# Butterfly weights of the first layer: two rotating buffers become three, the load is asked for in the middle of a step, and three bias loads move behind them

## The chip, the cores and the metric

The kernel runs on one core of a Trainium2 chip. A core has five engines that follow their own instruction streams: TensorE (PE, with weight loads shown apart as PEld), VectorE (DVE), ScalarE (ACT), GpSimd (POOL) and SyncE (SP), which in this kernel issues nearly all DMA transfers. Times are device microseconds from the first to the last instruction of one execution. The kernel before was run three times: 4143.59, 4148.38 and 4153.01 us; its time is the median, 4148.38 us. One further execution was profiled.

## The reference, cut to what matters

Four layers act on x, 4096 tokens of 128 numbers. Each is `x + s * silu(g)` with s from an attention block and g from a feed-forward block. Only the first layer matters here. Its attention has 16 heads of 8 numbers, a causal mask over 256 tokens, and two relative-position terms that look up products of q and k with position vectors by the clipped distance of two tokens:

```python
relpos = jnp.clip(qi[None, :] - qi[:, None], -WIN + 1, 0) + (WIN - 1)
c2p = jnp.einsum('bnhd,whd->bhnw', q, rk)[:, :, qi[:, None], relpos]
p2c = jnp.einsum('bnhd,whd->bhwn', k, rq)[:, :, relpos, qi[None, :]]
logits = (c2c + c2p + p2c) / math.sqrt(hd * scale_factor)
```

Its feed-forward block has butterflies between two dense matrices. A butterfly of 512 numbers has 9 steps; step `stage` mixes pairs that stand 2**stage apart with four weights a pair:

```python
h = butterfly(jnp.einsum('bsd,dh->bsh', x, W_exp) + b_exp, up_weights, 512)
h = butterfly(jax.nn.gelu(h + up_bias, approximate=False), down_weights, 512)
y = jnp.einsum('bsh,hd->bsd', h, W_con) + b_con + down_bias
# one step:
na  = w[..., 0, 0] * a + w[..., 0, 1] * b
nb2 = w[..., 1, 0] * a + w[..., 1, 1] * b
```

Up to the gelu everything is linear, and so is everything behind it.

## The kernel before

Because of that linearity the kernel never applies a butterfly to tokens. It applies the nine steps once to the rows of `W_exp`, once to the single row `b_exp`, and, transposed and in reverse order, to the rows of `W_con` transposed; from then on the block is two dense products. That makes 27 steps, numbered 0 to 26 here: 0 to 8 for `wexp` (128 rows of 512), 9 to 17 for `bexp` (one row), 18 to 26 for `wconT` (128 rows). A step is done on POOL in two halves of three instructions (`stage`, L160 to L180): two products of 128x256 (L171), then their sum (L174). Its 1024 weights are loaded from DRAM by the SP queue and spread over the 128 partitions (`fetch`, L189 to L195, 512 KB written; one row for steps 9 to 17). The weight load of step k is called w(k) here. Loads and intermediate rows lie in the buffer `xn`, which holds the normalised input of the layer: `room` is a view of it, free after its transposes. Two weight buffers rotate: step n asks for w(n+1) before its own first product, and so w(k) has to wait until the last product of step k-2 has read the same buffer.

While POOL does this, the first layer's attention (`attn0`) runs on all engines. Its 64 items are numbered n = 4b + m: batch b of 16, and a group m of four heads. An item is scored, shifted, softmaxed and mixed: TensorE forms the scores of four heads (L382), adds straightened position terms (L393 to L395), DVE adds the second position term and takes the row maximum (L398 to L400), ACT takes exp (L403), TensorE turns the result (L409), ACT and DVE copy it out of PSUM (L412, L414), and TensorE mixes (L423) one item later. The position terms go through DRAM, where a slanted write does the lookup:

- **Band store (b, hh, i)**, for hh, i in 0, 1: TensorE forms a product (L346), ACT copies it to `a_es` (L354), and SP writes it slanted (L357), twice: first a `cs` write, then a `pc` write, 256 KB each. `a_es` has two buffers in all, so ACT's copy for one band store waits until the DMA writes of the band store before it have read theirs.
- **Band load (b, hh)**: SP reads four pieces back, two for `a_p` (L362, 768 KB, and L363, 512 KB) and two for `a_c` (L364, L365). `a_p` has two buffers: the load for (b, hh) waits until POOL's copies have read the load two before it.
- **Straightening copies** of item n: eight copies on POOL, two for each head (L373, L374), from `a_p`; the next `project_qk` adds four products on POOL (L326).

The band stores of batch b+1 stand in items 4b (h = 0 and 1) and 4b+1, its band loads in items 4b+2 and 4b+4. `next(aside, None)` puts one half of a butterfly step into the program after each item, and a loop behind the last item takes what is left. The engine of TensorE keeps the order in which the program is written (`manual_schedule` names PE alone). For all other engines and for the SP queue the framework lays down an order when the program is built, from its own estimates of when operands are ready. Each engine and the SP queue then follow their order strictly; an instruction that waits holds back everything behind it on the same engine or queue.

At the end, `done` (L212 to L227) adds the biases: `bf_bs` from the `bexp` row and `upb` (L215), and `bdn`, the sum of `bcon` and `dnb` on DVE (L226). Before the change these three are loaded at the start of the layer (L210), and the sum `bdn` stands early in DVE's order.

In short, for the SP queue: weight loads and band transfers share one queue, and weight loads wait for POOL.

Of the kernel before, what the change touches and what calls it, by code (L numbers as in the profile page):

```python
# [8 lines left out]
F32 = mybir.dt.float32  # L9
# [6 lines left out]
P = 128  # L16
# [17 lines left out]
class Net:  # L34
# [113 lines left out]
    def butterflies(self, c):  # L148

        nc, tc = self.nc, self.tc
        wup = c.tile([P, 512], F32, name="wup")
        wdn = c.tile([P, 4, D], F32, name="wdn")
        bup = c.tile([P, 4], F32, name="bup")
        bdn = c.tile([P, D], F32, name="bdn")
        room = self.xn.rearrange("p k d -> p (k d)")
        ws = [room[:, 1024 * i : 1024 * i + 1024] for i in range(2)]
        ys = [room[:, 2048 + 512 * i : 2560 + 512 * i] for i in range(2)]
        t = room[:, 3072:3584].rearrange("p (j n) -> p j n", j=2)  # L160
        ends = {"bexp": room[:1, 3584:4096], "wexp": wup}

        def stage(out, y, wt, s, down):
            step, rows = 1 << s, y.shape[0]
            w5 = wt[:rows].rearrange("p (n s i j) -> p n s i j", s=step, i=2, j=2)
            src = y.rearrange("p (n t s) -> p n t s", t=2, s=step)
            dst = out.rearrange("p (n t s) -> p n t s", t=2, s=step)
            for i in range(2):
                for j in range(2):
                    v = w5[:, :, :, j, i] if down else w5[:, :, :, i, j]  # L170
                    nc.gpsimd.tensor_tensor(  # L171
                        t[:rows, j, :].rearrange("p (n s) -> p n s", s=step), src[:, :, j, :], v, ALU.mult
                    )
                nc.gpsimd.tensor_tensor(  # L174
                    dst[:, :, i, :],
                    t[:rows, 0, :].rearrange("p (n s) -> p n s", s=step),
                    t[:rows, 1, :].rearrange("p (n s) -> p n s", s=step),
                    ALU.add,
                )
                yield  # L180

        def steps():
            plan = [
                (name, weights, s)
                for name, weights in (("wexp", "upw"), ("bexp", "upw"), ("wconT", "dnw"))
                for s in (range(8, -1, -1) if name == "wconT" else range(9))
            ]

            def fetch(n):  # L189
                name, weights, s = plan[n]  # L190
                w = self.a[weights][:, 1024 * s : 1024 * s + 1024]
                rows = self.a[name].shape[0]
                if rows > 1:
                    w = w.rearrange("o n -> (o n)").partition_broadcast(P)
                nc.sync.dma_start(ws[n % 2][:rows], w)  # L195

            fetch(0)
            for n, (name, _, s) in enumerate(plan):
                rows, q = self.a[name].shape[0], n % 9
                if q == 0:  # L200
                    y = ys[0][:rows]
                    nc.sync.dma_start(y, self.a[name])
                if n + 1 < len(plan):
                    fetch(n + 1)
                o = ends[name] if q == 8 and name in ends else ys[(q + 1) % 2][:rows]
                yield from stage(o, y, ws[n % 2][:rows], s, name == "wconT")
                y = o
            ends["wconT"] = y

        ub, b1, b2 = self.load(c, "upb"), self.load_bc(c, "bcon"), self.load_bc(c, "dnb")  # L210

        def done():  # L212
            with tc.tile_pool(name="bf", bufs=1) as sb, tc.tile_pool(name="bf_ps", bufs=1, space=PSUM) as ps:
                bs = sb.tile([1, 512], F32, name="bf_bs")
                nc.vector.tensor_tensor(bs, ends["bexp"], ub, ALU.add)  # L215
                pb = ps.tile([P, 4], F32, name="bf_pb")
                for j in range(4):
                    nc.tensor.matmul(
                        pb[:, j : j + 1], lhsT=bs[:, j * P : (j + 1) * P], rhs=self.ones[:1, :1], start=True, stop=True
                    )  # L220
                nc.vector.tensor_copy(bup, pb)
                pd = ps.tile([P, 4, D], F32, name="bf_pd")
                for j in range(4):
                    nc.tensor.transpose(pd[:, j, :], ends["wconT"][:, j * P : (j + 1) * P], self.ident)
                nc.vector.tensor_copy(wdn, pd)
                nc.vector.tensor_tensor(bdn, b1, b2, ALU.add)  # L226
            return wup, bup, wdn, bdn  # L227

        return steps(), done

    def attn0(self, c, w, bias, wv, wo, bv, bo, aside):
# [1821 lines left out]
```

## Time and profile before

| what | value |
|---|---|
| median of three runs | 4148.38 us (4143.59 to 4153.01) |
| profiled execution, its own time | 4153.89 us |
| its span | 4152.2 us, mean granted TensorE clock 0.95 |
| PE busy | 3626.3 us, 87% of the span |
| DVE / ACT / POOL busy | 72% / 51% / 46% |
| first layer's attention, first to last item's scores (L382) | 62.0 to about 738 us |
| butterfly steps on POOL (L171, L174) | 61.6 to 258.9 us |
| four items, from 16 to 20 (285.9 to 324.7 us) | 38.8 us |
| items 0 to 14 | 62.0 to 265.1 us, 14.5 us each |

The profile has a page for the whole span and answers for stretches of it. Busy time is counted for each engine; a waiting instruction is not busy. A line of a timeline gives the start, the busy time, the engine, the source line, the operation with what it writes and reads, how many were merged, and in brackets how long the engine had been idle before and what ended that. A line of the table of waits gives who waited for whom, the time in total, how often, and the longest. A line of windows gives, for one stretch, the busy time of PE, PEld, DVE, ACT and POOL with the number of instructions, then the granted TensorE clock, the share of the DMA engines' time and GB/s.

The SP queue's order of the program before, as it was built, in the stretch of the butterflies. S(b,hh,i) is a band store, L(b,hh) a band load with the source lines' last digit, w(k) a weight load, and in brackets the step whose last product it waits for:

```
w0, S(0,0,1), L(0,0), S(0,1,0), wexp, w1, S(0,1,1), L(0,1), w2[0], S(1,0,0), w3[1], w4[2], S(1,0,1),
L(1,0):23, S(1,1,0), L(1,0):4, S(1,1,1) with L(1,0):5, L(1,1):23, w5[3], w6[4], w7[5], w8[6], L(1,1):45,
w9[7], bexp[8], w10[8], S(2,0,0), w11[9], S(2,0,1) with L(2,0):2, w12[10], w13[11], L(2,0):3, S(2,1,0),
w14[12], S(2,1,1) with L(2,0):45, L(2,1):23, w15[13], w16[14], w17[15], w18[16], L(2,1):45, wconT[17], w19[17],
cs of S(3,0,0), w20[18], pc of S(3,0,0), w21[19], S(3,0,1), L(3,0):23, w22[20], w23[21], S(3,1,0),
L(3,0):4, S(3,1,1), L(3,0):5, L(3,1):23, w24[22], w25[23], w26[24], L(3,1):45, S(4,0,0), ...
```

POOL's order in the same stretch (k is a step with halves a and b, c(n.h) the two copies of item n and head h, K the four products of L326; a copy between two halves may stand between their instructions):

```
c0 c1 0ab 1ab c2.0 c2.1 K c2.2 c2.3 2ab 3a c3.0 3b c3.1 4ab c3.2 c3.3 c4 c5.0 5a c5.1 5b 6a c5.2 6b c5.3 7ab 8ab
c6.0 c6.1 K 9a c6.2 c6.3 9b 10ab 11ab c7.0 c7.1 12ab c7.2 13a c7.3 13b 14ab c8 c9.0 15a c9.1 15b 16a c9.2 16b c9.3 17ab
c10.0 c10.1 18a K 18b c10.2 19a c10.3 19b 20ab 21ab c11.0-2 22a c11.3 22b 23ab c12 24a c13.0 24b c13.1 25ab c13.2 26a c13.3 26b c14.0 ...
```

### The profile page before, as it was taken

Reading aid. Unit: us, or ns where it says so; the run is one execution under the profiler, and the core shown is the slowest. Engines: PE = TensorE matmul, PEld = TensorE weight load, DVE = VectorE, ACT = ScalarE, POOL = GpSimd, SP = SyncE. Lnnn points to the kernel's source line nnn. Section 1 sums busy time; section 2 is a strip of 40 time slices with the busy share of each in tenths; the row PEclk is TensorE's granted clock in tenths of the full one; section 3 lists DMA queues with packets and bytes.
Section 4 is the critical chain, followed back from the end, with each engine's and each line's share of the span. In section 5 each row is a group of like instructions: output and inputs, shape, how many; then the busy total and the mean of one; then the engine's idle time right before and its main releaser. Section 6 shows DMA issues by size and latency. Waiting matters only on the chain. (4 is left out here: it accounts for less than half of the span.)

```text
span 4152.2 us, 61413 instructions
## 1 busy us (share of the span) xinstructions
PE 3626.3 (87%) x21623; PEld 2323.1 (56%) x21623; DVE 2987.9 (72%) x6273; ACT 2126.9 (51%) x4623; POOL 1918.5 (46%) x1979
## 2 busy tenths in 40 slices
PE   5689999875999999999999999769788899899795
PEld 3467777543566666777777776546333333333353
DVE  5467767575888887666666667636888999999834
ACT  2356666642777775444545333223565665666322
POOL 5974444000444443433333100250789877777634
PEclk8899999986999999999999899979899999999998
DMA  8365554320000001000000300010111211121123
GB/s 301 126 212 182 195 194 175 42 78 6 1 1 1 1 1 42 1 1 1 1 1 1 115 1 1 7 35 1 65 66 66 84 64 66 75 82 62 52 81 100
DMA packets 87366, 268.90 MB, mean 65 GB/s; under 512 B 18176, under 2 KB 34088, under 8 KB 81555
## 3 DMA queue, kind: packets, MB, share of 16 engines
q1 hardware_dynamic: 80403, 255.46, 18.0%
q0 software_dynamic: 6656, 9.52, 0.7%
q8 instruction: 172, 2.82, 0.3%
q14 instruction: 135, 1.11, 0.1%
HBM read 192.96 MB, written 71.97 MB: 64 GB/s over the span
## 5 line engine op out<-in xcount | busy, mean ns | idle before, releaser
L1827 POOL TENSOR_TENSOR m_h<-m_B,m_dtu 128x1024 f32<-128x1024 f32 x256 | 597.5, 2358 | 108.2 <-PE m_y L1957 104.1
L1853 DVE TENSOR_TENSOR_SCAN m_h<-m_a,m_h 128x512 f32<-128x512 f32 x512 | 601.3, 1208 | 40.1 <-ACT m_a L1842 34.8
L1957 PE MATMUL m_y<-m_h,ident 128*128 128x512 f32 x1024 | 513.8, 631 | 24.0 <-DVE m_h L1953 23.5
L883 POOL TENSOR_TENSOR a_e<-a_e,a_sm 128x512 f32<-128x512 f32 x256 | 263.8, 1041 | 445.2 <-DVE a_sm L882 351.5
L1117 DVE SCALAR_TENSOR_TENSOR f_acc<-f_po,f_gate,f_acc 128x128 f32<-128x128 f32 x1024 | 287.6, 344 | 219.8 <-PE f_po L1112 152.3
L1112 PEld LDWEIGHTS f_po<-values_sb,f_h 128*128 128x128 f32 x2048 | 277.5, 198 | 207.9 <-issue 130.5
L1957 PEld LDWEIGHTS m_y<-m_h,ident 128*128 128x128 f32 x1024 | 184.1, 195 | 340.3 <-issue 246.1
L398 DVE TENSOR_TENSOR a_e<-a_s,a_c 128x384 f32<-128x384 f32 x256 | 216.3, 845 | 189.9 <-PE a_s L395 183.6
L1189 POOL TENSOR_TENSOR r_g<-r_t 128x256 f32<-128x256 f32 x256 | 183.5, 728 | 360.3 <-DVE r_t L1188 357.2
L1083 ACT ACTIVATE f_h<-f_ph 128x512 f32<-128x512 f32 x256 | 152.2, 596 | 384.4 <-PE f_ph L1081 310.9
L1112 PE MATMUL f_po<-values_sb,f_h 128*128 128x128 f32 x2048 | 282.3, 283 | 71.5 <-ACT f_h L1083 46.6
L1220 ACT ACTIVATE r_e<-r_s,r_mx 128x256 f32<-128x256 f32 x512 | 208.0, 474 | 260.9 <-DVE r_mx L1214 260.8
L1953 DVE TENSOR_TENSOR m_h<-m_h,m_C 128x1024 f32<-128x1024 f32 x256 | 307.1, 1200 | 26.0 <-PE m_C L1863 26.0
L1188 DVE TENSOR_TENSOR r_t<-r_pp,trig_sb 128x512 f32<-128x512 f32 x256 | 169.5, 683 | 207.5 <-PE r_pp L1179 206.3
L876 ACT ACTIVATE a_e<-a_e,a_mx 128x256 f32<-128x256 f32 x512 | 255.1, 500 | 54.6 <-DVE a_sm L882 48.2
L1081 PE MATMUL f_ph<-xnT_sb,keys_sb 128*128 128x512 f32 x512 | 273.6, 618 | 0.4 <-ACT f_gate L1048 0.4
L403 ACT ACTIVATE a_e<-a_e,a_mx 128x128 f32<-128x128 f32 (+1 forms) x512 | 218.6, 453 | 93.0 <-DVE a_mx L399 65.0
L1208 PE MATMUL r_s<-pe_sb,r_g 128*128 128x256 f32 x1024 | 260.7, 388 | 0.0
L373 POOL COPY a_st<-a_p 128x192 f32<-128x192 f32 x256 | 135.7, 532 | 243.5 <-PE a_s L394 160.9
L1842 ACT ACTIVATE m_a<-m_dt,bA_sb 128x510 f32<-128x510 f32 x256 | 170.9, 686 | 141.3 <-DVE m_h L1853 140.4
L1863 PE MATMUL m_C<-m_dbc,ident 32*128 32x512 f32 x512 | 149.1, 655 | 96.6 <-DVE m_h L1953 92.3
L1842 ACT ACTIVATE m_a<-m_dt,fA_sb 128x510 f32<-128x510 f32 x256 | 169.9, 685 | 101.3 <-DVE m_h L1853 100.4
(476 smaller groups left out, 8227.5 us busy)
## 6 DMA issues: line engine op xcount, KB each, us to landing
m_B<-m_rows SPq DMA_DIRECT2D x32, 2048.0 KB
a_p<-pc SPq DMA_DIRECT2D x32, 768.0 KB
a_c<-cs SPq DMA_DIRECT2D x32, 768.0 KB
cs<-a_es SPq DMA_DIRECT2D x64, 256.0 KB
pc<-a_es SPq DMA_DIRECT2D x64, 256.0 KB
a_p<-pc SPq DMA_DIRECT2D x32, 512.0 KB
a_c<-cs SPq DMA_DIRECT2D x32, 512.0 KB
cs<-bg SPq DMA_DIRECT2D x8, 768.0 KB
```

The lines of the kernel that those rows point to most:

```text
L403: nc.scalar.activation(e[:, cols], e[:, cols], AF.Exp, bias=mx[:, i : i + 1])
L876: nc.scalar.activation(e[:, i, :], e[:, i, :], AF.Exp, bias=mx[:, i : i + 1], accum_out=sm[:, i : i + 1])
L883: nc.gpsimd.tensor_tensor(e, e, bc(sm, S), ALU.mult)
L1081: nc.tensor.matmul(ph, lhsT=keys[:, e, :], rhs=self.xnT[:, t * 512 : (t + 1) * 512], start=True, stop=True)
L1112: nc.tensor.matmul(po[:, k, :], lhsT=hT[:, k * P : (k + 1) * P], rhs=values[:, e, :], start=True, stop=True)
L1117: nc.vector.scalar_tensor_tensor(acc[:, n, :], po[:, k, :], gate[:, n, e : e + 1], acc[:, n, :], ALU.mult, ALU.add)
L1208: nc.tensor.matmul(s[h][:, i, :], lhsT=G[:, i * P : (i + 1) * P], rhs=w["pe"], start=False, stop=i == 1)
L1827: nc.gpsimd.tensor_tensor(h, st["B"][n // 8][:, m : m + 2, :], bc1(st["dtu"][:, k, :], 2), ALU.mult)
L1842: nc.scalar.activation(f[:, :, 1:], sts[d]["dt"][:, k, :].rearrange("p (b t) -> p b t", b=2)[:, :, 1:], AF.Exp, scale=w[work[d][1]]["A"][: ...
L1853: nc.vector.tensor_tensor_scan(h[:, j, :], ready.pop(0), h[:, j, :], 0.0, op0=ALU.mult, op1=ALU.add)
L1953: nc.vector.tensor_tensor(h, h, sts[d]["C"], ALU.mult)
L1957: nc.tensor.matmul(sts[d]["y"][k], lhsT=net.ident, rhs=h[:, j, :], start=False, stop=n + j == N - 1)
```

## The change

Three things change in `butterflies`. A third weight buffer is added, a tile `bf_w` of its own (4 KB a partition), so that the weights rotate over three buffers and w(k) waits for the last product of step k-3 instead of k-2. Step n asks for w(n+2) between its two halves; before, it asked for w(n+1) ahead of its first half. And `upb`, `bcon` and `dnb` are no longer loaded at the start of the layer into tiles of their own, but after the last step, into the first 768 columns of `room`.

```diff
-        ws = [room[:, 1024 * i : 1024 * i + 1024] for i in range(2)]
+        ws = [room[:, 1024 * i : 1024 * i + 1024] for i in range(2)] + [c.tile([P, 1024], F32, name="bf_w")]
...
-                nc.sync.dma_start(ws[n % 2][:rows], w)
+                nc.sync.dma_start(ws[n % 3][:rows], w)
 
             fetch(0)
+            fetch(1)
             for n, (name, _, s) in enumerate(plan):
...
-                if n + 1 < len(plan):
-                    fetch(n + 1)
                 o = ends[name] if q == 8 and name in ends else ys[(q + 1) % 2][:rows]
-                yield from stage(o, y, ws[n % 2][:rows], s, name == "wconT")
+                half = stage(o, y, ws[n % 3][:rows], s, name == "wconT")
+                yield next(half)
+                if n + 2 < len(plan):
+                    fetch(n + 2)
+                yield from half
                 y = o
             ends["wconT"] = y
-
-        ub, b1, b2 = self.load(c, "upb"), self.load_bc(c, "bcon"), self.load_bc(c, "dnb")
+            nc.sync.dma_start(ub, self.a["upb"])
+            for b, name in ((b1, "bcon"), (b2, "dnb")):
+                nc.sync.dma_start(b, self.a[name].rearrange("o n -> (o n)").partition_broadcast(P))
+
+        ub, b1, b2 = room[:1, 0:512], room[:, 512:640], room[:, 640:768]
```

The order on TensorE and ACT stays as it was. The orders that the framework lays down for the SP queue and POOL are new ones:

```
SP:   w0, S(0,0,1), L(0,0), S(0,1,0), w1, S(0,1,1), L(0,1), wexp, w2, S(1,0,0), w3[0], w4[1], S(1,0,1),
L(1,0):23, S(1,1,0), L(1,0):4, S(1,1,1) with L(1,0):5, L(1,1):23, w5[2], w6[3], w7[4], w8[5], w9[6], L(1,1):45,
w10[7], bexp[8], w11[8], S(2,0,0), w12[9], S(2,0,1) with L(2,0):2, w13[10], w14[11], L(2,0):3, S(2,1,0),
w15[12], S(2,1,1) with L(2,0):45, L(2,1):23, w16[13], w17[14], w18[15], w19[16], wconT[17], w20[17], L(2,1):45,
w21[18], w22[19], cs of S(3,0,0), w23[20], pc of S(3,0,0), w24[21], cs of S(3,0,1), L(3,0):2, pc of S(3,0,1),
w25[22], w26[23], L(3,0):3, S(3,1,0), L(3,0):4, S(3,1,1), L(3,0):5, L(3,1):23, upb, bcon, dnb, L(3,1):45, S(4,0,0), ...

POOL: c0 c1 c2.0 c2.1 K c2.2 0a c2.3 0b 1ab 2ab 3a c3.0 3b c3.1 4ab c3.2 c3.3 c4 c5.0 5a c5.1 5b 6a c5.2 6b c5.3 7ab 8ab
c6.0 c6.1 K 9a c6.2 c6.3 9b 10ab 11ab 12ab c7.0 c7.1 13ab c7.2 14a c7.3 14b 15ab c8 c9.0 16a c9.1 16b 17a c9.2 17b c9.3 18ab 19ab
c10.0 20ab c10.1 K 21a c10.2 21b c10.3 22ab 23ab 24ab c11.0 c11.1 25a c11.2 25b c11.3 26ab c12 c13 ...
```

On DVE one instruction moves: `bdn` (L226), which reads the loaded `bcon` and `dnb`, stood ahead of the attention and now stands directly ahead of item 11's first sum (L398). Lines behind the change have numbers higher by 6 in the changed file; the numbers of the kernel before are used throughout.

## The prediction

> **What bounds the kernel now.** I read the page for the place, then the windows, the waits of that stretch, and the timelines of SP, PE and POOL. The page shows no engine that bounds the whole span; the edit can act only where the butterflies run, at the head. Windows around it:
>
> ```profile
> 62.00:265.00 203.00, 139.98 (x1117) 111.40 (x1116) 111.24 (x211) 84.12 (x202) 187.90 (x281) 0.86 0.54 182
> 304.00:343.00 39.00, 35.93 (x330) 29.00 (x329) 27.43 (x61) 23.96 (x60) 17.73 (x36) 1.00 0.55 191
> ```
>
> With butterflies PE (first busy column) is busy 140 of 203 us and POOL (fifth) 188; without them 36 and 18 of 39. So PE sets the pace later, 38.8 us per four items, and items 0 to 14 take 203 us where 14 x 9.7 = 136 would do: 67 us are lost. The waits of 55 to 265 us, SP's own first, say to whom:
>
> ```profile
> SPq L195 <- POOL xn_sb L171: 98.6, 18, 11.3
> ...
> ACT a_es L354 <- DMA cs<-a_es: 62.8, 9, 12.8
> ...
> PE a_pp L440 <- ACT a_es L354: 27.8, 3, 10.3
> ```
>
> Weight loads hold the SP queue 98.6 us until POOL lets their buffer go; band stores queue behind; ACT waits to refill `a_es` behind them, and PE for ACT. From item starts (L382), item 1 to 2 takes 22.5 us, 5 to 6 31.2, 9 to 10 34.9, where the later pattern takes 11.1: these three stalls hold 55 of the 67 us. The third, on PE and then on SP:
>
> ```profile
> 200.38 1.44 PE L440 MATMUL a_pp<-ident,a_ot 128*128 128x128 f32 x4 [10.32 <-ACT a_es L354]
> 211.12 1.11 PE L440 MATMUL a_pp<-ident,a_ot 128*128 128x128 f32 x4 [9.30 <-ACT a_es L354]
> 219.81 0.55 PE L409 MATMUL a_pt<-ident,a_e 128*128 128x128 f32 x3 [1.80 <-ACT a_t L412]
> 222.81 0.94 PE L382 MATMUL a_s<-a_km,a_qt 32*128 32x128 f32 x16
> ```
>
> ```profile
> 205.60 0.33 SPq L195 DMA_DIRECT2D xn_sb<-in_dnw  x1
> 205.98 0.42 SPq L357 DMA_DIRECT2D pc<-a_es  x1
> 212.07 0.33 SPq L195 DMA_DIRECT2D xn_sb<-in_dnw  x1
> 212.50 0.38 SPq L357 DMA_DIRECT2D cs<-a_es  x1
> 212.97 0.39 SPq L357 DMA_DIRECT2D pc<-a_es  x1
> 213.45 0.46 SPq L362 DMA_DIRECT2D a_p<-pc  x1
> 218.23 0.32 SPq L363 DMA_DIRECT2D a_p<-pc  x1
> ```
>
> Each band write leaves 0.4 us behind a weight load. The load at 212.07 waited for step 19's last product; the store S(3,0,1) behind it lands at 218.2 (the L363 load waits for it) and item 10 begins at 222.81. POOL's prices:
>
> ```profile
> 197.88 1.66 POOL L171 TENSOR_TENSOR xn_sb<-xn_sb 128x256 f32<-128x256 f32 x2 [2.52 <-DMA xn_sb<-in_wconT]
> 199.52 3.63 POOL L326 TENSOR_SCALAR a_km<-a_kt,hmask_sb 128x256 f32<-128x256 f32 x4
> 215.49 1.66 POOL L171 TENSOR_TENSOR xn_sb<-xn_sb 128x256 f32<-128x256 f32 x2
> 217.23 0.73 POOL L174 TENSOR_TENSOR xn_sb<-xn_sb 128x256 f32<-128x256 f32 x1
> 218.04 1.67 POOL L171 TENSOR_TENSOR xn_sb<-xn_sb 128x256 f32<-128x256 f32 x2
> ```
>
> A half step is 2.55 us (215.49 to 218.04), a step 5.1, its last product done 4.2 after its start; one head's copies 0.85; L326 3.6. POOL has under 11 us of gaps from 61 to 265 us: its order is its timetable.
>
> **The change part by part.**
>
> *What the third buffer buys.* w(k) waits for step k-3, not k-2. But the load also stands one earlier in the program, and the built SP order shows the two cancelling: before each band transfer up to wconT stands w(j+1) where w(j) stood, behind the same step. S(2,0,1) waited for step 9 and does; S(2,1,0) for 11; S(2,1,1) for 12. Only S(1,0,1) moves from step 2 to 1. So a wait is worth what POOL's timetable and the SP order make it.
>
> *Start.* The three bias loads leave SP at 9.11 to 11.50; the fills behind start at 13.74. Bounds: 0 to 2.4 us earlier. I take 1.5, since two of them stood waiting for landings that others now wait for.
>
> *First stall.* In the new POOL order item 2's first copies and L326 stand before step 0, and L326 waits for `a_kt` (DVE, done 69.6, now 68.1). So L326 ends 71.7, step 0 starts 72.6 (before: 61.61), and with early halves of 2.7 us (64.44 to 67.25 is 2.8) step 1's last product ends at 83.2. Before, step 2's let the load go at 84.00. One step less to wait for, one step later begun: gain 0.8 us.
>
> *Weights for step 5.* POOL is now a step behind, so item 3's copies end at 103.0, not 97.9. L(1,1)'s first load (SP 97.85) waits for them, for their `a_p` buffer; w(5) stands behind it. Before, w(5) landed at 108.36 and POOL waited 2.23 us for it. Now it is issued at about 103.8, after 768 and 512 KB loads, at the windows' 340 GB/s: landing about 111, POOL ready at 107. Lag of POOL's timetable: +2.7. Ends: -1.3 (POOL's own readiness alone) and +5.2 (the whole delay of the copies).
>
> *Second stall.* Same steps on both orders up to S(2,0,1): +2.7, item 6 at 157.5 against 154.8.
>
> *wconT.* Step 17's last product (192.98) comes 0.8 earlier in the set (one copy less) and 2.7 later: 194.9. The load landed 4.9 us after with 1.3 MB of band loads ahead, now gone; the shortest landing on SP's rows is 2.2 (write at 229.71, L363 at 231.87). I take 3: step 18 starts at 198.0 (before 197.88). Ends 197.1 and 199.8.
>
> *Third stall.* Here the orders part. S(3,0,1) stood behind w(21), step 19; now behind w(24), step 21. From step 18's start the new POOL order has three steps, the products of a fourth, three copies and L326: 3 x 5.1 + 4.2 + 3 x 0.85 + 3.6 = 25.6, so step 21 lets go at 223.6 instead of 212.07, +11.5. And L(3,0)'s 768 KB now goes ahead of the `pc` write: 0.79 MB / 340 GB/s = 2.3. PE's restart and item 10 come 13.7 later: 236.5. Ahead of that, item 8's copies stand a step later (181 against P 177), but the stall swallows it. S(3,1,0) moves behind w(26), step 23, at 223.6 + 0.8 + 0.85 + 5.1 + 4.2 = 234.6, before 222.3: +12.3, and a 512 KB load ahead: same lag, item 11 at 248.0.
>
> *`bdn`.* DVE now holds item 11's sums until `dnb` lands. It is issued behind L(3,1)'s loads, which wait for item 11's last copy: 234.6 + 0.8 + 5.1 + 5.1 + 4 x 0.85 = 249.0. Then 1.3 MB / 340 GB/s and 2.2: `bdn` at 255. Item 11's first sum would start at 236.14 + 13.7 = 249.9, so +5.3; PE waits with it for the turn's copy (L414) and the score banks. Ends 0 (sum already late) and +8.
>
> *What is given back.* POOL ends the butterflies by item 11 instead of 13. Items 12 to 16 took 43.6 us, the free pattern takes 38.8: 0 to 4.8, I take 2.4. Nothing more, since PE sets that pace.
>
> *Weighed against a rule.* At 78.08 DVE's L400 took 3.33 us, elsewhere 0.16, while POOL ran L326 and copies from 74.44 to 79.7. The Trainium skill (SBUF — State Buffer, section SBUF: two separate sides) says that DVE and GpSimd share a port pair under an exclusive lock, so that one blocks while the other holds it. By it the copies of items 12 and 13, now in one run beside item 11's softmax, would lock DVE out again, and nothing of the 2.4 us would come back.
>
> *Sum.* 13.7 + 5.3 - 2.4 = +16.6 us against the profiled execution's 4153.89: 4170.5. That execution lies 5.5 above the median shown, so I predict 4148.4 + 16.6 = 4165.
>
> **The rivals.** A difference under 0.2% (8.3 us) is about what a measurement of this kernel can't tell from none.
>
> 1. *Every wait a step shorter: faster.* If POOL keeps its old timetable, three buffers end each of the three stalls a step (5.1 us) sooner: -15.3, 4133. It decides when step 0 starts by 67 us, not 72.6, and S(3,0,1) is let go before 212. For it: 98.6 us of SP waits are there to be had. Against: both built orders. 8%.
>
> 2. *Eaten later: no change.* The lag of 13.7 stands, but `bdn`'s load lands in time, the 4.8 come back whole, and POOL's 8 us of gaps after 100 us (0.7, 0.2, 3.0, 2.2, 2.5) shrink by 3 or more: 13.7 - 4.8 - 3 = +6, 4154. For it: those gaps are waits on PE and on loads asked for late. Against: `dnb` queues behind 1.3 MB. 14%.
>
> 3. *`bdn` at its dearest.* The lag of step 5 is the full 5.2 and wconT lands at 199.8 (+4.3), `bdn` costs 8 and nothing returns: 13.7 + 4.3 + 8 = +26, 4174. 16%.
>
> **How the numbers follow.** My forecast, +9 to +21 (4157 to 4170 as its own range), has 62%. Slower by over 0.2%: forecast and rival 3, 78%; within: 14%; faster: 8%. The range leaves out rival 1 and the outer ends: 4151 to 4177.
>
> **What would show it.** Step 0's first product near 72.6 instead of 61.6; POOL waiting for an `upw` load near 107 to 111; item 6 near 157.5; a weight load on SP near 223.6 with the `cs` write behind it and PE idle longest before item 10, which starts near 236; a DVE gap ended by a DMA near 255; last butterfly sum near 255 with items 12 and 13 not yet copied; 38.8 us per four items from item 13 on. I am wrong if step 0 starts early (the timetable then runs ahead of every later step), if item 10 starts before 229, or if PE's pace beyond item 12 was set by POOL and drops below 9.7 us an item.

## The result and the profile after

The changed kernel takes 4170.24 us (median of 10 runs, 4161.47 to 4186.48); the kernel before, run beside it ten times, 4150.83 us. The ratio is 1.0043, with a 95% interval of 1.0028 to 1.0058: 17.9 us slower (12 to 24), where 4165 against 4148 was predicted. The profiled execution took 4169.41 us (span 4167.7), 15.5 more than the profiled execution of before.

The same two windows as before (columns: sum, then PE, PEld, DVE, ACT, POOL busy, clock, DMA share, GB/s; the second one lies an us later, on the same four items of the later pattern):

```profile
62.00:265.00 203.00, 121.53 (x914) 96.22 (x910) 87.12 (x175) 69.38 (x169) 182.22 (x270) 0.79 0.48 160
305.00:344.00 39.00, 35.96 (x338) 29.02 (x334) 27.55 (x62) 23.98 (x61) 17.73 (x36) 1.00 0.54 190
```

The later pattern is what it was: 36 and 18 us of 39, and 38.8 us per four items. At the head PE now does 122 us of work in 203 where it did 140. The items say where (start of the first scores, us):

| item | before | after | later by |
|---|---|---|---|
| 0 | 62.0 | 60.4 | -1.6 |
| 2 | 96.3 | 97.1 | 0.8 |
| 6 | 154.8 | 158.7 | 3.9 |
| 9 | 187.9 | 192.7 | 4.8 |
| 10 | 222.8 | 237.5 | 14.7 |
| 11 | 234.2 | 248.1 | 13.9 |
| 12 | 242.3 | 265.9 | 23.6 |
| 16 | 285.9 | 304.7 | 18.8 |
| 63 | 737.2 | 755.5 | 18.3 |

Two steps make most of the loss, item 9 to 10 and item 11 to 12; 4.8 us are there by item 9 already, and as much comes back from 12 to 16. The waits between 55 and 265 us (engine, tile, line, releaser: us in total, times, longest):

```profile
SPq L195 <- POOL xn_sb L171: 96.1, 17, 10.8
...
ACT a_es L360 <- DMA cs<-a_es: 81.0, 9, 21.4
...
PE a_pp L446 <- ACT a_es L360: 34.4, 3, 19.2
...
DVE bdn L232 <- DMA xn_sb<-in_dnb: 8.3, 1, 8.3
```

SP's waits for POOL are as long as before (96.1 against 98.6 us), ACT's waits for the `cs` writes of band stores are 18 us longer, and DVE has a new one. The third stall, on PE and on the SP queue:

```profile
214.05 1.44 PE L446 MATMUL a_pp<-ident,a_ot 128*128 128x128 f32 x4 [19.20 <-ACT a_es L360]
219.91 1.12 PE L446 MATMUL a_pp<-ident,a_ot 128*128 128x128 f32 x4 [4.42 <-ACT a_es L360]
...
232.47 0.90 PE L415 MATMUL a_pt<-ident,a_e 128*128 128x128 f32 x3 [6.08 <-ACT a_t L418]
...
237.47 0.94 PE L388 MATMUL a_s<-a_km,a_qt 32*128 32x128 f32 x16
...
258.47 0.90 PE L415 MATMUL a_pt<-ident,a_e 128*128 128x128 f32 x3 [7.58 <-DVE a_t L420]
```

```profile
214.44 0.33 SPq L195 DMA_DIRECT2D bf_w<-in_dnw  x1
214.86 0.39 SPq L363 DMA_DIRECT2D pc<-a_es  x1
223.64 0.33 SPq L195 DMA_DIRECT2D xn_sb<-in_dnw  x1
224.06 0.38 SPq L363 DMA_DIRECT2D cs<-a_es  x1
224.54 0.38 SPq L368 DMA_DIRECT2D a_p<-pc  x1
224.97 0.49 SPq L363 DMA_DIRECT2D pc<-a_es  x1
```

The load at 223.64 is w(24), let go by step 21; S(3,0,1) leaves behind it, with L(3,0)'s first piece between its two writes. PE, which stood idle 19.20 us ahead of the first row shown, starts item 10 at 237.47. Its last row is held by the new wait, on DVE:

```profile
256.64 0.56 DVE L232 TENSOR_TENSOR bdn<-xn_sb 128x128 f32<-128x128 f32 x1 [8.27 <-DMA xn_sb<-in_dnb]
257.12 0.83 DVE L404 TENSOR_TENSOR a_e<-a_s,a_c 128x384 f32<-128x384 f32 x1
```

### The profile page after: what moved, and what is told of

It is laid out like the page before. It is cut to its first block, busy times and chain, and to the rows that moved or that the text cites. A ratio compares the mean times of both kernels' runs of the same rounds, so it can differ in the third digit from the quotient of the medians.

```text
span 4167.7 us, 61422 instructions
## 1 busy us (share of the span) xinstructions
PE 3631.3 (87%) x21623; PEld 2327.5 (56%) x21623; DVE 2972.4 (71%) x6273; ACT 2126.4 (51%) x4623; POOL 1918.0 (46%) x1979
## 3 DMA queue, kind: packets, MB, share of 16 engines
q1 hardware_dynamic: 80403, 255.46, 18.1%
## 5 line engine op out<-in xcount | busy, mean ns | idle before, releaser
L404 DVE TENSOR_TENSOR a_e<-a_s,a_c 128x384 f32<-128x384 f32 x256 | 216.6, 846 | 206.9 <-PE a_s L401 204.6
```

## The experiments

The kernel before took 4089 us in the median beside e1 to e4, 4147 beside e5 to e8, 4151 beside e9 to e11 and 4093 beside e12, each group on another chip. So only ratios to the runs beside a kernel are compared, and times within the first layer's attention (item 63 starts at 737.2 us in before) are taken from the profiles.

**What was not run.** Asking for a load between the two halves of a step changes nothing in what is built. With two buffers and the request behind the first half, every engine and SP get the instruction order of before, instruction for instruction; with three buffers and the request two steps ahead, but ahead of the first half, they get the orders of e1. What is left of the change is the third buffer with a load two steps ahead, the biases, and one thing that is easily overlooked: `fetch(1)` now stands ahead of the load of the `wexp` rows.

### e1_bias_start: the biases back at the start

```diff
-        ub, b1, b2 = room[:1, 0:512], room[:, 512:640], room[:, 640:768]
+        ub, b1, b2 = wdn[:1, :, :].rearrange(...), wup[:, 0:128], wup[:, 128:256]
+        nc.sync.dma_start(ub, self.a["upb"])
+        ...
+        nc.vector.tensor_tensor(bdn, b1, b2, ALU.add)
```

> After, with the three bias loads back at the start (in rows that are written later) and bdn formed there; SP and POOL orders otherwise those of after. Theory (the wait for dnb on DVE is a real loss of its own): item 11 to 12 falls from 17.8 to about 8.1 us as in before, the start costs 1.3 more, so 8 us less than after: about +10 us against before (+7 to +13). Rival (POOL's copies of item 12 would have been late anyway, bdn hidden): item 12 stays near 266, +18 to +20 against before.

Measured: 1.0025 (1.0013 to 1.0036), +10 us. Item 11 to 12 takes 8.1 us as in before, item 12 comes at 256.5 instead of 265.9: the wait for `dnb` was a loss of 9.7 us there. But item 12 to 13 takes 16.4 instead of 11.4, and at item 63 only 4.0 us are saved (751.5 against 755.5). What took the wait's place stands in DVE's timeline of e1, and in POOL's at the same time:

```profile
259.61 0.55 DVE L405 TENSOR_REDUCE a_mx<-a_e 128x3 f32<-128x384 f32 x1
260.19 3.85 DVE L406 TENSOR_TENSOR a_mx<-a_mx 128x1 f32<-128x1 f32 x1
263.97 0.47 DVE L328 TENSOR_SCALAR a_qt<-a_pp,a_qb 128x256 f32<-128x256 f32 x1
```

```profile
259.87 0.55 POOL L379 COPY a_st<-a_p 128x192 f32<-128x192 f32 x1
...
263.14 0.54 POOL L379 COPY a_st<-a_p 128x192 f32<-128x192 f32 x1
263.61 0.42 POOL L380 COPY a_st<-a_p 128x128 f32<-128x128 f32 x1
265.69 3.63 POOL L332 TENSOR_SCALAR a_km<-a_kt,hmask_sb 128x256 f32<-128x256 f32 x4 [1.66 <-DVE a_kt L330]
```

A minimum of two columns, 0.16 us in the median, lasts 3.85 us and ends when POOL's run of copies ends (264.03). In before the same instruction (L400) stands at item 14, and it is the longest of the whole stretch:

```profile
264.27 6.53 DVE L400 TENSOR_TENSOR a_mx<-a_mx 128x1 f32<-128x1 f32 x1
270.72 0.83 DVE L398 TENSOR_TENSOR a_e<-a_s,a_c 128x384 f32<-128x384 f32 x1
```

```profile
270.37 0.42 POOL L374 COPY a_st<-a_p 128x128 f32<-128x128 f32 x1
```

It ends at 270.80, with the last of 16 copies that follow each other without a gap. After has no minimum over 1.2 us between 55 and 300 us (before four, 13.8 us beyond their 0.16): there POOL makes these copies from 254.56 to 259.6, when DVE first stands waiting for `dnb` and then has sums, a copy and a reduction to do. Of these only `bdn`, itself a sum of two tensors from SBUF, took longer than elsewhere (0.56 us, 0.29 in e2). So the hold that is gone at item 14 is what was given back from item 12 to 16.

### e2_bias_only: the biases alone

```diff
             ends["wconT"] = y
-        ub, b1, b2 = self.load(c, "upb"), self.load_bc(c, "bcon"), self.load_bc(c, "dnb")
+            nc.sync.dma_start(ub, self.a["upb"])
+            ...
+        ub, b1, b2 = room[:1, 0:512], room[:, 512:640], room[:, 640:768]
```

> Before, with only the bias loads moved behind the butterflies. They then stand behind L(3,1)'s last load, which before issued at 245.4, and bdn stands in DVE's order after the second row maximum of item 12 (248.9). Theory (the cost is not in moving the biases but in where the third buffer's order puts them): dnb lands near 250, DVE's next sum starts at 250.3 anyway; 1.3 gained at the start, 1.2 on SP ahead of S(4,0,0): 0 us against before (-3 to +3). Rival (the biases cost the same wherever they come late): +8 to +10 us.

Measured: 1.0014 (1.0001 to 1.0026), +6 us; item 63 is 6.4 later. The theory's number was wrong. SP's rows and DVE's:

```profile
243.29 0.42 SPq L368 DMA_DIRECT2D a_c<-cs  x1
255.88 0.25 SPq L209 DMA_DIRECT2D xn_sb<-in_upb  x1
256.19 0.33 SPq L211 DMA_DIRECT2D xn_sb<-in_bcon  x1
256.57 0.42 SPq L211 DMA_DIRECT2D xn_sb<-in_dnb  x1
257.04 0.43 SPq L360 DMA_DIRECT2D cs<-a_es  x1
```

```profile
259.67 0.29 DVE L229 TENSOR_TENSOR bdn<-xn_sb 128x128 f32<-128x128 f32 x1 [12.83 <-DMA xn_sb<-in_dnb]
```

The loads stand 12 us on the queue, because the biases' rows lie in the first weight buffer, and with two buffers step 26 still reads it, until 255.9. With three it is step 24. I had overlooked that wait. Moving the biases late costs in either kernel, here even more at the place (item 12 to 13: 23.5 us against 11.8), and 4.5 us come back because the hold at item 14 goes. Of the two numbers given, 0 and +8 to +10, neither is right.

### e3_wexp_first: the start's order of before

```diff
             fetch(0)
-            fetch(1)
             ...
                     nc.sync.dma_start(y, self.a[name])
+                if n == 0:
+                    fetch(1)
```

> As e1_bias_start, but the load of the wexp rows is written ahead of the second weight load. POOL's built order then has step 0 where before had it (ahead of item 2's copies); SP's order from w(2) on is that of after. Theory (POOL is full, so its timetable sets the second and third stall, and the first stall's gain is eaten): step 0 starts near 61, the first stall (item 1 to 2) shrinks from 24 to 11-14 us, but item 6 comes at 154 to 156 and item 10, which still waits for step 21, at 232 to 235; 12 to 16 in 38.8: 3 us less than e1, +7 us against before (+3 to +10). Rival (each stall is worth its own length): the 11 us of the first stall stay, -1 us or less against before.

Measured: 1.0022 (1.0012 to 1.0033), +9 us; in the profile item 63 is 7.1 later than in before. Step 0 starts at 61.56. Item 2 starts at 88.6 (before 96.3, e1 97.2), item 5 at 116.5 (123.6, 124.3), and item 6 at 153.9 (154.8, 158.8): the eight us of the first stall, now 14.9 us long where 11 to 14 were expected, are gone again at the second, as the theory has it. At the third stall S(3,0,1) still stands behind w(24), but leaves earlier:

```profile
217.69 0.33 SPq L195 DMA_DIRECT2D xn_sb<-in_dnw  x1
218.11 0.38 SPq L364 DMA_DIRECT2D cs<-a_es  x1
```

POOL is a step ahead here (step 18 at 192.5 instead of 198.4), w(24) is let go at 217.69 instead of 223.64, and item 10 starts at 232.0 (232 to 235 expected): 5.5 us earlier than in after, 9.2 later than in before. Items 12 to 16 take 43.6 us and not the 38.8 expected: a minimum is held again, for 3.68 us at 253.30. The timed runs can't tell e3 from e1 (0.03% between them); the profiles put 7.2 us between them at item 63.

### e9_third_buffer_alone: asked for where before asks

```diff
             fetch(0)
-            fetch(1)
             ...
-                if n + 2 < len(plan):
-                    fetch(n + 2)
+                if n + 1 < len(plan):
+                    fetch(n + 1)
```

The diff is against e1 (three buffers, biases at the start), and the whole step follows in one piece as in before.

> Before with the third weight buffer alone: each load is asked for one step ahead, ahead of the step's first product, as before; biases at the start. In the built order S(2,0,1) then stands behind the load that waits for step 10, S(3,0,1) behind w(25), which waits for step 22 (before: 19; after and e3: 21). Theory (the framework fills the queue with as many weight loads as buffers allow, and each one more is a step of POOL ahead of the band stores): third stall one step of 5.1 us longer than in e3, item 10 near 237; about +12 us against before (+6 to +18). Rival (a third buffer by itself lets the queue through): 0 or less.

Measured: 1.0006 (0.9993 to 1.0019), +2 us, the same as before within what can be measured; item 63 5.6 later. SP holds two weight loads ahead of S(3,0,1) (the row is a pair; it starts with the first load at 217.65 and ends with w(25) behind step 22):

```profile
217.65 6.10 SPq L195 DMA_DIRECT2D xn_sb<-in_dnw  x2
223.84 0.38 SPq L360 DMA_DIRECT2D cs<-a_es  x1
```

Item 10 at 236.4 is what the theory gave (237), but the sum is not: items 10 to 12 take 16.4 us where before takes 19.5, and 12 to 16 take 38.9 instead of 43.6. The third stall ends 4.4 us later than in e3, and more than half of the 13.6 us that item 10 is late comes back behind it. Part of that is the hold at item 14 again: before has it, e9 has no minimum over 1.2 us behind item 7. The rival fails as well: with the third buffer by itself the SP queue still waits, only behind a later step.

### e4_hand_order and e7_hand_order_before: POOL and SP in the program's order

```diff
-            ctx.enter_context(tc.manual_schedule(engines={mybir.EngineType.PE}))
+            ctx.enter_context(
+                tc.manual_schedule(engines={mybir.EngineType.PE, mybir.EngineType.Pool, mybir.EngineType.SP}))
```

e4 makes this edit in after, e7 in before.

> After, with POOL and the SP queue kept in the order in which the program is written, like TensorE: one half step after each item, weight loads one per two items, asked for long after their buffer is free. Theory (the loss is the early order that the framework lays down, not the butterflies' work or their traffic): POOL needs 4 x 3.8 + 3.7 + 4 x 2.6 = 29 of 38.8 us per four items, no stalls, items at 9.7 us from the first: 64 us less than before (4080 to 4100 us), bands stores never behind a weight load that waits. Rival A (the traffic of the weights or the POOL work itself costs it): within 10 us of before. Rival B (a half step ahead of the four products of the next batch makes each batch late by 2.6 us): 15 x 2.6 = 39 us given back, about -25 us against before.

> Before (two buffers, load asked for one step ahead, biases at the start) with POOL and SP in the program's order. Theory (with one half step an item a load is asked for an item after its buffer is free, so the third buffer buys nothing): the same as e4 within 6 us, -27 to -40 against before. Rival (the third buffer is needed because SP would stop behind step k-2): 10 us or more above e4.

Measured: e4 0.9921 (0.9909 to 0.9934), -32 us; e7 0.9922 (0.9905 to 0.9939), -32 us. The waits of e4's SP queue for weight buffers, now over the 640 us from 60 to 700, and the window of the head:

```profile
SPq L195 <- POOL xn_sb L171: 2.4, 2, 2.1
```

```profile
62.00:265.00 203.00, 180.24 (x1595) 144.25 (x1596) 142.31 (x299) 118.37 (x291) 133.52 (x240) 0.99 0.59 207
```

96 us of waiting are 2.4, none of the three stalls is left (items 1 to 12 take 107.6 us, before 168.5), and PE does 180 us of work in the window where after does 122. Two buffers do as well as three: with one half step per item a load is asked for when its buffer has long been read. So the loss is the order that the framework lays down, and not the work or the traffic of the butterflies (rival A); whether it is the order on the SP queue or on POOL, e4 can't say, since both were kept by hand. The size was wrong: item 63 comes 41 us earlier and not 64, since items now take 10.1 us and not 9.7, and the timed 32 us lie nearer to rival B's 25. Its reason is not borne out by e11 below, which moves the four products and gains nothing in the attention. Where a batch is slow, DVE's and POOL's timelines show the hold again:

```profile
321.27 3.00 DVE L406 TENSOR_TENSOR a_mx<-a_mx 128x1 f32<-128x1 f32 x1
```

```profile
321.30 0.51 POOL L379 COPY a_st<-a_p 128x192 f32<-128x192 f32 x1
...
323.74 0.51 POOL L379 COPY a_st<-a_p 128x192 f32<-128x192 f32 x1
324.20 0.40 POOL L380 COPY a_st<-a_p 128x128 f32<-128x128 f32 x1
```

It ends at 324.27, with the seventh of eight copies (324.25).

### e5_hand_two_maxima, e12_hand_scalar_minimum and e10_before_two_maxima: the hold

```diff
-                nc.vector.tensor_reduce(mx[:, 0:3], e.rearrange(...), AX.X, ALU.max, negate=True)
-                nc.vector.tensor_tensor(mx[:, 1:2], mx[:, 1:2], mx[:, 2:3], ALU.min)
+                for i in range(2):
+                    nc.vector.tensor_reduce(mx[:, i : i + 1], e[:, P * i : P + 2 * P * i], AX.X, ALU.max, negate=True)
```

That is e5 (in e4) and e10 (in before). e12 is e4 with one instruction of another form:

```diff
-                nc.vector.tensor_tensor(mx[:, 1:2], mx[:, 1:2], mx[:, 2:3], ALU.min)
+                nc.vector.tensor_scalar_min(mx[:, 1:2], mx[:, 1:2], mx[:, 2:3])
```

> e4_hand_order with the row maximum taken in two reductions on DVE (one for each group of columns that has its own maximum) in place of one reduction and a minimum of two 128x1 columns; POOL and SP orders the same as in e4. Theory (DVE's minimum is held as long as POOL runs without a gap: six holds of 1.3 to 3.3 us in e4, 15.5 us together, each ahead of a slow item): the holds are gone, no DVE instruction of the maximum takes over 0.6 us, about half of the 15.5 us was on the path: 8 us less than e4, about -40 us against before (-36 to -50). Rival (the holds are covered by PE's own pace): like e4, -29 to -35.

> e4_hand_order with the same minimum of two 128x1 columns, but with the second column given as a scalar for each partition instead of as a second tensor; POOL and SP orders the same as in e4. Theory (it is the form with two tensors from SBUF that is held while POOL runs): no such instruction takes over 0.6 us (e4: six over 1.2, the longest 3.3), item 63 near that of e5 (686), -38 to -50 us against before. Rival (any short DVE instruction at that place is held): holds of 1.3 to 3.3 us again, item 63 near 696, -28 to -36.

> Before with the row maximum taken in two reductions instead of one and a minimum of two columns; the framework moves single copies and band transfers past a neighbour, nothing else. Theory (DVE's minimum was held by POOL's run of copies for 6.5 us at item 14, and that is the 4.8 us which after had back): item 14 to 15 falls from 12.7 to 8.2 us, -5 us against before (-10 to -1). Rival (the hold is covered): within 2 us of before.

Measured: e5 0.9886 (0.9865 to 0.9907), -47 us, item 63 at 686.0 (e4 696.1). e12 0.9864 (0.9842 to 0.9887), -56 us, item 63 at 683.4. e10 0.9973 (0.9961 to 0.9984), -11 us: item 14 to 15 takes 8.2 us instead of 12.7, as expected, and item 63 comes 7.2 earlier; the median lies just past the -10 that was given. The group of the minimum over the attention, in e4 and then in e12 (count: shortest/median/longest in ns, first and last start):

```profile
L406 DVE TENSOR_TENSOR a_mx<-a_mx x256: 112/160/3276, 65.0 to 705.3; 128x1 f32<-128x1 f32 x128
```

```profile
L406 DVE TENSOR_SCALAR a_mx<-a_mx x256: 159/211/225, 64.4 to 692.5; 128x1 f32<-128x1 f32 x128
```

Same place, same work, same orders on POOL and SP: with two tensors up to 3.3 us, with a tensor and a scalar for each partition never over 0.23. So it is the form that is held, and the rival (any short instruction there) falls. The six holds over 1.2 us add up to 15.5 us beyond their 0.16 in e4; without holds item 63 comes 12.7 us earlier (696.1 to 683.4). The gain of e12 is larger than the 38 to 50 us given.

### e6_hand_sp and e8_pool_queue: which queue

```diff
-            ctx.enter_context(tc.manual_schedule(engines={mybir.EngineType.PE}))
+            ctx.enter_context(tc.manual_schedule(engines={mybir.EngineType.PE, mybir.EngineType.SP}))
```

```diff
-                nc.sync.dma_start(ws[n % 3][:rows], w)
+                nc.gpsimd.dma_start(ws[n % 3][:rows], w)
```

> After, with only the SP queue kept in the program's order; POOL's order stays with the framework, which now places the steps near where their weights come (two or three in a row, the last ahead of item 45's copies). Theory (the loss is weight loads that stand ahead of band transfers and wait): SP waits under 10 us for weight loads, no stall over 15 us between items, -25 to -40 us against before. Rival (POOL's own order, several halves in a row ahead of an item's copies, is what delays): at most 15 us less than before.

> After, with the weight loads issued by POOL instead of SP, so that no band transfer can stand behind them; the framework then puts all 27 steps ahead of item 10's copies on POOL. Theory (POOL full is a limit of its own: 27 x 5.1 us of steps, 11 x 3.8 of copies and 3 x 3.6 make 190 us up to item 10, where the free pattern has 107, and loads on POOL add their issue): item 10 starts at 245 to 275 against 222.8 in before, +15 to +50 us in the end. Rival (only the SP queue is the loss): faster than before by 20 us or more.

Measured: e6 0.9935 (0.9918 to 0.9953), -27 us: the SP queue's order alone gives most of what e4 gave. SP waits 0.4 us for weight buffers; but three steps between items are still over 15 us (15.5, 17.2 and 18.1), which was not expected. POOL's order changed with it: the last step ends at 602.6 us, in after at 254.6.

e8 1.0059 (1.0042 to 1.0077), +24 us, within the range given; POOL is busy 183 of the 194 us between items 0 and 10, PE 104, and item 10 starts at 258.9:

```profile
65.00:259.00 194.00, 103.89 (x795) 81.90 (x794) 85.38 (x151) 61.13 (x147) 183.26 (x281) 0.76 0.44 148
```

But the rows give another reason than the theory's full POOL. PE's longest idle time there ends with DVE, DVE's ends with `dnb`, and the biases waited on SP:

```profile
237.34 0.90 PE L415 MATMUL a_pt<-ident,a_e 128*128 128x128 f32 x3 [27.53 <-DVE a_t L420]
...
235.78 0.29 DVE L232 TENSOR_TENSOR bdn<-xn_sb 128x128 f32<-128x128 f32 x1 [28.91 <-DMA xn_sb<-in_dnb]
...
230.56 0.25 SPq L212 DMA_DIRECT2D xn_sb<-in_upb  x1
```

`upb` lands in the first weight buffer, which step 24 reads until 230.53. The loads of the `bexp` and `wconT` rows (L203) are on SP too and wait for POOL as the weight loads did:

```profile
SPq L203 <- POOL xn_sb L171: 54.0, 2, 28.1
```

They leave at 117.84 and 182.93, with band transfers behind them. So the queue is held three times, by the rows of `bexp`, the rows of `wconT` and the biases, and e8's three longest steps, item 2 to 3 (33.8 us), 6 to 7 (27.4) and 8 to 9 (41.0), each end soon after one of these holds. So e8 took the weight loads off the queue and did not free it: it got the forecast time for another reason, and it refutes neither its rival nor the theory.

What e4, e6 and e8 have in common is a reading, not a result: the framework puts 27 steps, 138 us of POOL, ahead of the copies of item 10 (e8), 12 (after) or 14 (before), and any load on SP that waits for one of them holds the band transfers behind it. In e6 the queue's order also spreads the steps, so how much of its 27 us is the free queue and how much the spread is open. A run with POOL's order by hand and the framework's order on SP would tell, and there is none.

### e11_hand_late_masks: the masked products later

```diff
-                for m in range(4):
-                    nc.gpsimd.tensor_scalar_mul(km[:, m, :], kt, hm[:, m : m + 1])
+                kr[b] = kt
+            def mask_k(b):
+                ...
                 ...
                 (1, 1): [(lambda b: bands(b, 1, 0), 1)],
+                (1, 2): [(mask_k, 1)],
                 (1, 3): [(lambda b: bands(b, 1, 1), 1)],
```

> e5_hand_two_maxima with the four masked products of the next batch on POOL written two items' heads later (behind the copies of the item after next instead of ahead of the next item's). Theory (in the program's order POOL stands idle 7 us a batch for `a_kt` with the next item's copies behind it, and then runs late into the item after; with that gone a batch takes 38.8 to 39.5 us as in the free pattern): item 63 at 672 to 678 instead of 686, 10 us less than e5: about -54 us against before (-46 to -64). Rival (the half steps themselves are what makes an item longer): the same as e5 within 4 us.

Measured: 0.9862 (0.9842 to 0.9881), -57 us, but item 63 at 687.7, as in e5 (686.0): within the stretch that the edit touches the rival holds, and the intervals of the two ratios overlap, though the -57 us taken alone lie in the theory's range. What keeps a batch at 39 to 44 us there stays open; the longest gap that I followed was PE's 3.35 us at 362.6, behind ACT's wait for a band store's writes, and no run tests it.

e11 and e12 take 1.4% less than before, after 0.4% more; e12 is two statements away from after.

## Why the prediction was right, point by point

- **Start** (-1.5): the first fill left 1.3 us earlier, item 0 came 1.6 earlier. Right.
- **First stall** (step 0 at 72.6, gain 0.8): step 0 began at 73.33, w(4) was let go at 84.32 against 84.00. So 0.3 us of loss in place of 0.8 of gain. The mechanism held: one step less to wait for, one step later begun. e3 adds the cause (step 0 starts late only because w(1) went ahead of the `wexp` rows) and that a gain at this stall, as in rival 1, would not have lasted.
- **Weights for step 5** (landing about 111, lag +2.7) and **second stall** (item 6 at 157.5): POOL waited until 111.63, lag 3.3; item 6 at 158.7. The row:

```profile
111.63 0.87 POOL L171 TENSOR_TENSOR xn_sb<-xn_sb,bf_w 128x256 f32<-128x256 f32 x1 [4.05 <-DMA bf_w<-in_upw]
```

- **wconT** (step 18 at 198.0): 198.42, after a gap of 1.30 us for the rows. Right.
- **Third stall** (w(24) let go at 223.6, item 10 at 236.5, step 23's last product 234.6, item 11 at 248.0): 223.64, 237.5, 234.49 and 248.1. Right to 1 us; this term, 13.7 predicted and 14.7 measured, is the heart of it. For the release of S(3,0,1), 11.6 us later (223.64 against 212.07), the count of steps between step 18 and step 21, with the prices of a half step, a copy and L326 (now L332), was enough. Behind it two errors cancel, and that part is luck: PE goes on 12.7 us later (232.47 against 219.81) and not 13.7, but then needs 5.00 us to item 10 where before needed 3.00 for the same work, at a granted clock (third from last) of 0.59 against 1.00, which no step had. After, then before:

```profile
232.47:237.47 5.00, 5.00 (x27) 3.47 (x27) 0.00 (x0) 1.82 (x5) 4.69 (x7) 0.59 0.52 97
```

```profile
219.81:222.81 3.00, 3.00 (x28) 2.14 (x28) 0.69 (x2) 1.83 (x5) 2.92 (x5) 1.00 0.79 307
```

- **`bdn`** (+5.3, bounds 0 and 8): 9.7, outside its bounds. `dnb` landed 1.6 us later than 255, the first sum of item 11 began at 257.12 and not at 249.9, so 7.2 us on DVE; the other 2.5 are PE's restart behind it, which the step left out: from that sum to item 12 after takes 8.8 us and e1 6.2, again at a lower clock (0.63 against 1.00). e1 shows the 9.7 gone when the load stands at the start.
- **Given back** (-2.4, bounds 0 and 4.8): 4.8. The step took it for POOL's lighter load. It was one instruction of before, the minimum held for 6.53 us at 264.27 (in e10, which has no such minimum anywhere, item 14 to 15 takes 8.2 us instead of 12.7).
- **The weighed rule**: the Trainium skill (SBUF — State Buffer, section SBUF: two separate sides) has DVE and GpSimd share a port pair under an exclusive lock. By it nothing would have come back, since the copies in one run would lock DVE out. A hold that fits the rule is there (e1: 3.85 us at just that place, e12: it goes with the form). In after it didn't show, because DVE stood waiting for `dnb` when the run of copies began and had its next minimum only behind it. Where the page has the lock held "for the whole instruction", the traces show DVE shut out over many of POOL's instructions, 16 copies in before; there the measurement decides.

The mechanism held; the closeness of the total is in part luck, since the errors nearly cancel: +1.0 at the third stall, +4.4 at `bdn`, -2.4 at what came back, and -0.8 and -0.5 that no step had (item 10 to 11, and behind item 16): 18.3 us at item 63 where the sum had 16.6. The profiled executions as a whole differ by 15.5; the other 2.8 lie behind the attention, where nothing was changed. Rival 1 (4133) failed where it said it would, at a step 0 that starts late and at S(3,0,1) let go at 223.64. Rival 2 was right that the 4.8 come back whole and wrong that `dnb` lands in time. Rival 3 was nearest on `bdn` (8 against 9.7) and wrong about the rest.

From the profiles the 18.3 us divide as: 4.0 for the biases (after against e1), 7.2 for w(1) ahead of the `wexp` rows (e1 against e3), 7.1 for the third buffer with loads two steps ahead (e3 against before). Taken in another order the parts differ (the biases alone, e2, cost 6.4), and each includes minima that are held in one kernel and not in the other (6.53 us in before, 3.85 in e1, 3.68 in e3). The timed ratios agree with the order of after, e1 and e3, but are too wide to confirm each part.

## What to carry to other kernels

Another buffer for a load on a shared, ordered queue doesn't shorten a wait if the load also moves one place ahead: count, in the built order, which step of the slow engine stands in front of each transfer that others need. Taking some of these loads to another queue is not enough either, as long as others that wait for the same engine stay (e8). Work that fills the gaps of another loop must be kept in these gaps by an order that holds; left to the framework it went all to the front, and an order by hand was worth 0.8% where this change cost 0.4%. If a tiny DVE instruction with two tensor operands shows a long duration, look at what POOL runs at that time, and change the form.

## What the runs showed of the hardware

- A DVE minimum of two 128x1 columns took 0.16 us in the median and up to 6.53 us while POOL ran copies or products back to back. Long holds are few: of 134 minima in before that began while a POOL instruction ran, four lasted over 1.2 us and the others at most 0.89. In all thirteen holds over 1.2 us in before, e1 and e4 its end lies within 0.03 us behind the end of one of POOL's instructions. Which of them lets it go is not settled: some are followed by a gap of 0.08 us, others by the next copy at once. The sums with one operand in PSUM and the row reductions (L404, L405) kept their 0.85 and 0.54 us, and the same minimum with a scalar for each partition stayed under 0.23 (e12).
- TensorE's granted clock was 0.59 over the 5.0 us behind an idle time of 6.08 us (after, 232.47) and 0.63 over the 7.4 us behind one of 7.58 us (258.47), against 1.00 behind 1.80 us in before (219.81).
- A weight load issued on POOL's queue (e8) held POOL for 0.58 us in the row at 64.62 us, and for 0.53 to 0.61 in all but the first of the 27; on SP the median row is 0.33.
- The same kernel before had medians from 4089 to 4151 us over the five groups of runs.
